# Linear attention: q formed transposed with its norm applied at the output rows, and x (Wv W_out) computed beside k

## The chip, the cores and the metric

The kernel runs on one core of a Trainium2 chip. A core has a matrix engine (TensorE, PE in the profile; PEld is its loading of weights), a vector engine (VectorE, DVE), an activation engine (ScalarE, ACT), GpSimd (POOL), and SyncE (SP), which here issues DMAs. Each engine takes its instructions in a fixed order and waits on semaphores for the others. Products land in PSUM[...]. The metric is the device time of one execution in microseconds.

## The reference

The program is a small vision tower on four images: a tokenizer, which gives 784 distinct rows of 256 channels per image (each row appears three times in the output), softmax attention across images, a mixture of six experts with two chosen per row, then linear attention, and a second mixture of experts. The change touches only the linear attention of layer 1. It computes, for x the layer norm of h:

```python
qkv = x @ W_qkv + b_qkv
q, k, v = jnp.split(qkv, 3, axis=2)
q = q - jnp.mean(q, axis=2, keepdims=True)
k = k - jnp.mean(k, axis=2, keepdims=True)
q2 = q * q
k2 = k * k
q2s = jnp.sum(q2, axis=2, keepdims=True)
k2s = jnp.sum(k2, axis=2, keepdims=True)
k2 = _l2_normalize(k2 / (k2s + EPS_DIV), axis=-2)
q2 = _l2_normalize(q2 / (q2s + EPS_DIV), axis=-1)
kv = jnp.einsum('bnc,bnd->bcd', k2, v)
t2 = jnp.einsum('bnc,bcd->bnd', q2, kv) / math.sqrt(N)
attn = v + t2
return attn @ W_out + b_out        # and then h = h + this
```

The norm of k2 runs over the rows of an image, that of q2 over the channels of one row.

## The kernel before

All arithmetic is fp32. The 784 rows of an image are 7 tiles of 112 rows; a unit is 4 or 3 tiles of one image, so there are eight units (0 to 7), two per image. h holds all 28 tiles in SBUF.

The expert stage ahead of the linear attention processes 30 blocks of 256 rows, one after another: each is fetched, transposed (turned), taken through two hidden layers (hidden) and written back to DRAM (rows_back). In its later part, the loop at L1483, VectorE and SyncE run in the order in which the code is written (manual_schedule); the other engines, and everything after that loop, are ordered by the compiler's scheduler at build time. centred_weights (L623) subtracts from the q and k weights and biases their means over the output channels, so that q and k need no mean subtracted later; it is called inside that loop.

For linear attention, fetch(u) (L1406) gathers each row's two expert results with indirect DMAs, issued by POOL, into one of three ys buffers. stats_one (L1423) adds them, weighted, to h and takes mean and variance; normalise (L1441) makes the normalised rows xa, and, once the weights of layer 1 exist, adds the output bias to h (residual, L1459). x_t (L1465) transposes xa to lxT: channels on the partitions, rows along the free dimension. copy_out (L77) gives the copies out of PSUM in turn to ScalarE and VectorE.

q_k (L1604) multiplies lxT by the q and k weights, 512 columns at a time, rows on the partitions (pqk); VectorE adds the bias, ScalarE squares both halves in place and sums each row, and squares q's half once more into a scratch tile (junk) for the sum of q's fourth powers. scales (L1637) turns the sums into factors: uk is k's squares scaled, and q's squares are scaled in place on VectorE. fold (L1660) adds up the squares of uk over rows. q_t (L1671) transposes the scaled q squares to lqT. k_x (L1676) forms k's product with x (pukx) and the norm over rows (pn), and scales the product to g; g_t transposes it and kv_out (L1714) multiplies it by Wvo, so that kvo holds kv @ W_out. rows_out (L1728) accumulates x @ Wvo and lqT @ kvo in one PSUM bank (pout) and adds the result to h.

Wvo = Wv @ W_out, its bias bvo and the output bias are made by layer1_weights (L639): four transposes (pwv), a copy to WvT by VectorE, two products (pwvo) copied by ScalarE, and one for the bias (pbvo). It is called in the loop at L1751, in step u = 1. That loop runs over the units in a pipeline: step u handles q and k of unit u, k_x and kv_out of the image that is complete, rows_out of unit u - 2, and the statistics of unit u + 1.

## Time and profile before

| | us |
|---|---|
| median of 3 runs | 810.28 |
| lowest and highest run | 808.37, 810.49 |
| profiled execution | 810.54 |
| its span, first to last instruction | 808.8 |
| linear attention, first product to last (pqk at 501.38 to the end of pout) | 162.1 |
| TensorE busy in the span | 739.7 |

The profile is of one execution. It lists, for each engine, busy time and instructions; stretches of time show where an engine is full; the groups name the line, the engine, the tiles written and read, the shape and the count, and then what ended the idle time before them. A TensorE product in fp32 is listed as two instructions, so that 28 tiles of pqk with two products each appear as 112. Groups of the linear attention, by shape, in 470 to 665 us of the span (busy us, mean ns, then idle time before):

```profile
L1620 PE MATMUL pqk<-Wqkv,lxT 128*112 128x512 f32 x112 | 49.7, 594 | 0.5 <-ACT lxT L81 0.5
L1735 PE MATMUL pout<-Wvo,lxT 128*112 128x256 f32 x112 | 29.0, 380 | 0.0
L1740 PE MATMUL pout<-kvo,lqT 128*112 128x256 f32 x112 | 28.8, 380 | 0.0
L1694 PE MATMUL pukx<-xa,uk 112*128 112x258 f32 x112 | 25.9, 384 | 0.0
L300 PE MATMUL pt<-ident,qk 112*128 112x112 f32 x56 | 7.0, 268 | 0.0
...
L1429 DVE SCALAR_TENSOR_TENSOR h<-ys,wk,h 112x256 f32<-112x256 f32 x48 | 21.8, 467 | 3.7 <-DMA ys<-yrows,pos 3.6
L1624 DVE TENSOR_TENSOR qk<-pqk,bqkv 112x512 f32<-112x512 f32 x28 | 19.1, 685 | 9.2 <-PE pqk L1620 9.1
L1653 DVE TENSOR_SCALAR qk<-qk,ss 112x256 f32<-112x256 f32 x28 | 8.4, 360 | 0.1
L1746 DVE TENSOR_TENSOR h<-pout,h 112x512 f32<-112x512 f32 x12 | 8.2, 685 | 8.5 <-PE pout L1740 8.5
...
L1628 ACT ACTIVATE qk<-qk 112x256 f32<-112x256 f32 x56 | 22.8, 407 | 27.7 <-DVE qk L1624 25.2 <-DMA yrows<-yb 2.3
L1629 ACT ACTIVATE junk<-qk 112x256 f32<-112x256 f32 x28 | 11.2, 400 | 0.0
```

A mean of one instruction holds its whole latency; neighbours on an engine overlap, so the distance from start to start is shorter than the duration listed.

### The profile page before, as it was taken

Reading aid. Unit: us, or ns where it says so; the run is one execution under the profiler, and the core shown is the slowest. Engines: PE = TensorE matmul, PEld = TensorE weight load, DVE = VectorE, ACT = ScalarE, POOL = GpSimd, SP = SyncE. Lnnn points to the kernel's source line nnn. Section 1 sums busy time; section 2 is a strip of 40 time slices with the busy share of each in tenths; the row PEclk is TensorE's granted clock in tenths of the full one; section 3 lists DMA queues with packets and bytes.
Section 4 is the critical chain, followed back from the end, with each engine's and each line's share of the span. In section 5 each row is a group of like instructions: output and inputs, shape, how many; then the busy total and the mean of one; then the engine's idle time right before and its main releaser. Section 6 shows DMA issues by size and latency. Waiting matters only on the chain. (4 is left out here: it accounts for less than half of the span.)

```text
span 808.8 us, 10871 instructions
## 1 busy us (share of the span) xinstructions
PE 739.7 (91%) x3524; PEld 501.2 (62%) x3524; DVE 504.0 (62%) x1618; ACT 334.1 (41%) x789; POOL 131.0 (16%) x148
## 2 busy tenths in 40 slices
PE   5779996999788887999999999799999999999996
PEld 3645554555555655887888887475776775555553
DVE  4618776586767986546445746699975655554441
ACT  0326776355376475443222322527544503222221
POOL 4100000000006350760012030775000000000000
PEclk9889997999999988999999999899999999999999
DMA  8999991000002167442334334232000003333333
GB/s 204 371 419 421 420 420 46 1 0 1 1 0 63 36 225 237 143 147 92 105 97 132 94 109 128 85 87 69 1 1 1 1 20 89 90 94 94 94 91 90
DMA packets 58183, 97.39 MB, mean 120 GB/s; under 512 B 14519, under 2 KB 48494, under 8 KB 53262
## 3 DMA queue, kind: packets, MB, share of 16 engines
q1 hardware_dynamic: 50832, 80.52, 28.9%
q0 software_dynamic: 6112, 14.01, 6.0%
q10 hardware_dynamic: 1182, 2.16, 1.1%
q8 instruction: 28, 0.46, 0.2%
q14 instruction: 29, 0.24, 0.1%
HBM read 30.93 MB, written 65.74 MB: 120 GB/s over the span
## 5 line engine op out<-in xcount | busy, mean ns | idle before, releaser
L947 POOL DMA_INDIRECT xrows<-xn,pos x56 | 59.8, 1068 | 274.6 <-ACT kq L711 233.3
L1415 POOL DMA_INDIRECT ys<-yrows,pos x56 | 57.2, 1021 | 141.9 <-DMA yrows<-yb 125.8
L1219 PE MATMUL pb<-xTb,own 128*128 128x256 f32 x240 | 58.8, 389 | 3.8 <-DVE r L810 1.6
L1225 ACT ACTIVATE hb<-pb,own 128x256 f32<-128x256 f32 x74 | 35.1, 475 | 56.2 <-PE pb L1219 47.8
L1219 PE MATMUL pb<-hb,own 128*128 128x256 f32 x240 | 57.1, 380 | 0.3 <-DVE hb L1227 0.3
L1236 PE MATMUL pyb<-own,hb 128*128 128x256 f32 x240 | 57.0, 380 | 0.2 <-ACT hb L1225 0.2
L1219 PEld LDWEIGHTS pb<-xTb,own 128*128 128x128 f32 x240 | 44.6, 194 | 12.5 <-ACT hb L1225 1.9
L517 PE MATMUL pw<-Wall,pT 128*112 128x512 f32 x112 | 51.0, 610 | 0.0
L1620 PE MATMUL pqk<-Wqkv,lxT 128*112 128x512 f32 x112 | 49.7, 594 | 0.5 <-ACT lxT L81 0.5
L1236 PEld LDWEIGHTS pyb<-own,hb 128*128 128x128 f32 x240 | 45.4, 190 | 6.7 <-ACT hb L1225 0.6
L1219 PEld LDWEIGHTS pb<-hb,own 128*128 128x128 f32 x240 | 43.3, 190 | 5.9 <-DVE hb L1227 0.9
L300 PE MATMUL pt<-ident,xn 112*128 112x112 f32 x224 | 34.6, 286 | 12.5 <-DVE xn L540 6.8
L309 PE MATMUL pe<-xT,eW 128*128 128x448 f32 x112 | 45.2, 546 | 0.0
L1242 DVE TENSOR_TENSOR yb<-pyb,eb 128x512 f32<-128x512 f32 x30 | 20.7, 691 | 39.2 <-PE pyb L1236 38.8
L1209 ACT COPY xTb<-ptb 128x512 f32<-128x512 f32 x30 | 17.5, 584 | 64.0 <-PE ptb L1205 64.0
L300 PEld LDWEIGHTS pt<-ident,xn 112*128 112x128 f32 x224 | 27.0, 151 | 26.9 <-ACT xn L824 9.5
L1227 DVE TENSOR_SCALAR hb<-pb,own 128x256 f32<-128x256 f32 x46 | 22.1, 481 | 29.5 <-PE pb L1219 29.5
L517 PEld LDWEIGHTS pw<-Wall,pT 128*112 128x112 f32 x112 | 20.1, 182 | 26.2 <-issue 22.9
L320 PE MATMUL pwo<-Wo,oT 128*112 128x256 f32 x112 | 29.0, 413 | 7.5 <-DVE oT L776 6.7
L736 DVE SCALAR_TENSOR_TENSOR prod<-kq 128x784 f32<-128x784 f32 x32 | 30.3, 969 | 7.4 <-ACT kq L711 5.2
L1620 PEld LDWEIGHTS pqk<-Wqkv,lxT 128*112 128x112 f32 x112 | 19.3, 177 | 24.8 <-issue 23.0
L1628 ACT ACTIVATE qk<-qk 112x256 f32<-112x256 f32 x56 | 22.8, 407 | 27.7 <-DVE qk L1624 25.2
(360 smaller groups left out, 1502.6 us busy)
## 6 DMA issues: line engine op xcount, KB each, us to landing
xrows<-nothing SPq DMA_DIRECT2D x19, 1024.0 KB, 20.2
yrows<-nothing SPq DMA_DIRECT2D x19, 1024.0 KB
out_dram<-h SPq DMA_DIRECT2D x26, 336.0 KB, 3.8
xb<-xrows SPq DMA_DIRECT2D x30, 256.0 KB, 2.7
yrows<-yb SPq DMA_DIRECT2D x30, 256.0 KB, 2.2
ew<-in_L_ffn_expert_w_dram SPq DMA_DIRECT2D x6, 768.0 KB, 11.4
wb<-wd SPq DMA_DIRECT2D x28, 112.0 KB, 3.5
img<-in_x_dram SPq DMA_DIRECT2D x2, 588.0 KB
```

What stands on the lines that cost most here:

```text
L300: nc.tensor.transpose(pt[:, j * TT : (j + 1) * TT], xn[:, j, c * P : (c + 1) * P], ident[:TT, :TT])
L309: nc.tensor.matmul(pm[: wcols.stop - wcols.start, :n], w[:, c, wcols], xT(c), start=(c == 0), stop=(c == chunks - 1),)
L320: nc.tensor.matmul(pm[:, i, :], xT(c, t), w[:, c, :], start=(c == 0), stop=(c == chunks - 1))
L517: nc.tensor.matmul(pm, pTf[:, c, cut(t0 + j, 1)], Wall[:, c, :], start=(c == 0), stop=(c == 1))
L736: nc.vector.scalar_tensor_tensor(prod, qTs[s][:, o, :], 1.0, kT[:, o, t * SEQ : (t + 1) * SEQ], ALU.mult, ALU.mult, accum_out=atts[s][:, o ...
L947: put = nc.gpsimd.indirect_dma_start(out=xrows[:, :], out_offset=bass.IndirectOffsetOnAxis(ap=pos[:, k, t0 + j : t0 + j + 1], axis=0), in_ ...
L1219: nc.tensor.matmul(pm, wm[:, c, o * P : (o + 1) * P], src[:, c, :], start=(c == 0), stop=(c == 1),)
L1225: nc.scalar.activation(dst[:, o, :], pm, AF.Relu, bias=b)
L1236: nc.tensor.matmul(pm[:, t, :], src[:, c, t * P : (t + 1) * P], wm[:, c, :], start=(c == 0), stop=(c == 1),)
L1415: got = nc.gpsimd.indirect_dma_start(out=y[:, j, k, :], out_offset=None, in_=yrows[:, :], in_offset=bass.IndirectOffsetOnAxis(ap=pos[:, k, ...
L1620: nc.tensor.matmul(pqk, xT[:, c, cut(j, 1)], Wqkv[:, c, : 2 * D], start=(c == 0), stop=(c == 1),)
L1628: nc.scalar.activation(half, half, AF.Square, accum_out=ss[:, j, i : i + 1])
```

## The change

q is no longer formed beside k. q_of(u) forms it transposed, the weights standing still and the rows moving, two products of up to 448 columns for each half of the channels; ScalarE adds the bias column bq as it squares the result into lqT, and squares that again into q4. norms(u) sums q4 over the channels with a stationary block of 32 columns of ones (pq4, one column group per tile), copies the sums to qn, turns them into columns by a product with a strided view of the identity (pqn), and takes the reciprocal of the root (rq). It is called one step later than q_of. q's squares stay unscaled: rows_out multiplies the product with kvo by rq as it adds it to h (pqo).

k_of(u) forms k alone in unit 0. From unit 1 on, Wvo stands in the place of the v weights in Wqkv, so k and x @ Wvo come out of one product of 512 columns (pk); VectorE adds the first half to the bias and the second half to h. Unit 0 makes x @ Wvo in rows_out (pxo).

layer1_weights is called at the end of step 0 and copies WvT on ScalarE. The columns of bv (bvs) and of q's bias (pbq, bq) are made inside the block loop. The statistics of unit 2 and later are taken after k of the whole unit; a dependency that orders without a semaphore puts the adds of stats_one behind the last reciprocal of scales(1) for unit 2, and then behind the last add of the unit before. q_t, the junk tile and the scaling of q's squares are gone.

The diff, cut to its core:

```diff
...
-    def layer1_weights():
+    def q_bias():
+        pb = ps_tile("pbq")
+        for c in range(2):
+            nc.tensor.matmul(
+                pb[:, c : c + 1], bqkv[:1, c * P : (c + 1) * P], ones[:1], start=True, stop=True
+            )
+        return pb
+    def bias_columns():
+        bvs = w1p.tile([P, 2, P], F32, tag="bvs", name="bvs")
+        for k in range(2):
+            nc.vector.tensor_copy(bvs[:, k, :], col("bv", k).to_broadcast([P, P]))
+        return bvs
+    def layer1_weights(bvs):
         WvT = w1p.tile([P, 2, D], F32, tag="WvT", name="WvT")
         pt = ps_tile("pwv").rearrange("p (k i) -> p k i", k=2)
         for k in range(2):
...
-        nc.vector.tensor_copy(WvT, pt)
-        Wvo = w1p.tile([P, 2, D], F32, tag="Wvo", name="Wvo")
+        nc.scalar.copy(WvT, pt)
+        Wvo = Wqkv[:, :, 2 * D :]
...
-        bvs = w1p.tile([P, 2, P], F32, tag="bvs", name="bvs")
-        for k in range(2):
-            nc.vector.tensor_copy(bvs[:, k, :], col("bv", k).to_broadcast([P, P]))
...
+    bq = w1p.tile([P, 2], F32, tag="bq", name="bq")
...
     lw = []
+    behind = []
     def stats_one(u, j):
...
         for k in range(2):
-            nc.vector.scalar_tensor_tensor(
+            got = nc.vector.scalar_tensor_tensor(
                 h[:, t, :], ys[u][:, j, k, :], wk[:, k, t : t + 1], h[:, t, :],
                 ALU.mult, ALU.add,
             )
+            for name in behind if u > 1 else ():
+                tc.add_manual_dep(
+                    got.ins, name,
+                    mybir.DependencyInfo(
+                        mybir.DependencyClass.NoSync, mybir.DependencyReason.DATA
+                    ),
+                    reason="order",
+                )
+        if u > 1 and j == units[u][2] - 1:
+            behind[:] = [got.ins.name]
...
                 hidden(i, 1)
             if i == NEARLY + 1:
                 centred_weights()
+                bvs = bias_columns()
+            if i == NEARLY + 3:
+                pbq = q_bias()
+            if i == NEARLY + 5:
+                nc.vector.tensor_copy(bq, pbq[:, :2])
             for u in range(3):
                 if i - 1 == after[u]:
                     fetch(u)
...
     late = [early]
     lin = linear.enter_context(tc.tile_pool(name="lin", bufs=2, reuse_waits="tile"))
-    sumsof = {}
-    def q_k(u, j0, j1):
+    sumsof, q4s, rqs, with_v = {}, {}, {}, set()
+    ones32 = lin.tile([P, 32], F32, tag="ones32", name="ones32", bufs=1)
+    nc.vector.memset(ones32, 1.0)
+    def k_of(u):
+        b, j0, n = units[u]
+        if lw:
+            with_v.add(u)
+        xT = xTs[u]
+        kr = qks[u] = lin.tile([TT, GT, D], F32, tag="kr", name="kr")
+        ss = sumsof[u] = small.tile([TT, GT], F32, tag="ss", name="ss")
+        for two in halves(range(n)):
+            if not lw:
+                pk = mm_rows(two, lambda c, j: xT[:, c, cut(j, 1)], Wqkv[:, :, D : 2 * D], "pk")
+                nc.vector.tensor_tensor(
+                    kr[:, two[0] : two[-1] + 1, :], pk, over(bqkv[:, D : 2 * D], len(two)),
+                    ALU.add,
+                )
+            for j in two:
+                if lw:
+                    pk = ps_tile("pk")[:TT]
+                    for c in range(2):
+                        nc.tensor.matmul(
+                            pk, xT[:, c, cut(j, 1)], Wqkv[:, c, D:], start=(c == 0), stop=(c == 1)
+                        )
+                    nc.vector.tensor_tensor(kr[:, j, :], pk[:, :D], bqkv[:, D : 2 * D], ALU.add)
+                    ht = h[:, b * TPI + j0 + j, :]
+                    nc.vector.tensor_tensor(ht, pk[:, D:], ht, ALU.add)
+                nc.scalar.activation(
+                    kr[:, j, :], kr[:, j, :], AF.Square, accum_out=ss[:, j : j + 1]
+                )
+                if u > 1:
+                    stats_one(u + 1, j)
+        if u > 1:
+            next_stats(u)
+    def next_stats(u):
         n = units[u][2]
...
+        if u == 1:
+            for j in range(n):
                 stats_one(u + 1, j)
-        if j1 >= n and u:
+        if u:
             if u + 1 < len(units) and units[u + 1][2] > n:
                 stats_one(u + 1, n)
             normalise(u + 1)
+    def q_of(u):
+        n = units[u][2]
+        qT = qTs[u] = lin.tile([P, 2, GN], F32, tag="lqT", name="lqT", bufs=3)
+        q4 = q4s[u] = lin.tile([P, 2, GN], F32, tag="q4", name="q4", bufs=2)
+        for o in range(2):
+            pq = mm_t(
+                n * TT, Wqkv, slice(o * P, (o + 1) * P), lambda c: xTs[u][:, c, : n * TT], "pq1"
+            )
+            nc.scalar.activation(qT[:, o, : n * TT], pq, AF.Square, bias=bq[:, o : o + 1])
+        nc.scalar.activation(q4[:, :, : n * TT], qT[:, :, : n * TT], AF.Square)
+    def norms(u):
+        n = units[u][2]
+        q4 = q4s.pop(u)
+        pg = psum_s.tile([P, 512], F32, tag="pss", name="pq4")[: 32 * n, :TT]
+        for c in range(2):
+            for j in range(n):
+                nc.tensor.matmul(
+                    pg[32 * j : 32 * (j + 1), :], ones32, q4[:, c, cut(j, 1)],
+                    start=(c == 0), stop=(c == 1),
+                )
+        qn = small.tile([P, TT], F32, tag="qn", name="qn", bufs=2)[: 32 * n]
+        nc.scalar.copy(qn, pg)
+        pr = psum_s.tile([P, 512], F32, tag="pss", name="pqn")[:TT, :n]
+        nc.tensor.matmul(
+            pr, qn, ident.rearrange("p (j e) -> p j e", e=32)[: 32 * n, :n, 0],
+            start=True, stop=True,
+        )
+        r = rqs[u] = small.tile([TT, GT], F32, tag="rq", name="rq", bufs=4)
+        nc.scalar.activation(r[:, :n], pr, AF.Sqrt, bias=zero[:TT])
+        nc.vector.tensor_scalar(r[:, :n], r[:, :n], 1e-19, None, ALU.max)
+        nc.vector.reciprocal(r[:, :n], r[:, :n])
     def scales(u):
         b, j0, n = units[u]
-        qk = qks[u]
-        ss, s4 = sumsof.pop(u)
+        kr = qks.pop(u)
+        ss = sumsof.pop(u)
         nc.vector.tensor_scalar(ss[:, :n], ss[:, :n], 1e-7, None, ALU.add)
-        nc.scalar.activation(s4[:, :n], s4[:, :n], AF.Sqrt, bias=zero[:TT])
-        nc.vector.scalar_tensor_tensor(
-            ss[:, :n, 0], ss[:, :n, 0], 1e-12, s4[:, :n], ALU.mult, ALU.max
-        )
-        nc.vector.reciprocal(ss[:, :n], ss[:, :n])
+        last = nc.vector.reciprocal(ss[:, :n], ss[:, :n])
+        if u == 1:
+            behind.append(last.ins.name)
         uk = uks[u] = lin.tile([TT, GT, D], F32, tag="uk", name="uk", bufs=3)
         sq = lin.tile([TT, GT, D], F32, tag="sq", name="sq", bufs=1)
         for j in range(n):
-            nc.scalar.activation(uk[:, j, :], qk[:, j, D:], AF.Copy, scale=ss[:, j, 1:2])
-            nc.vector.tensor_scalar(
-                qk[:, j, :D], qk[:, j, :D], ss[:, j, 0:1], None, ALU.mult
-            )
+            nc.scalar.activation(uk[:, j, :], kr[:, j, :], AF.Copy, scale=ss[:, j : j + 1])
         for j in range(n):
             nc.scalar.activation(sq[:, j, :], uk[:, j, :], AF.Square)
...
-    def q_t(u):
-        n = units[u][2]
-        qT = qTs[u] = lin.tile([P, 2, GN], F32, tag="lqT", name="lqT", bufs=3)
-        transposed(qks.pop(u), n, lambda c, pt: copy_out(qT[:, c, : n * TT], pt))
...
     def rows_out(u):
         b, j0, n = units[u]
-        xT, qT, kvo = xTs.pop(u), qTs.pop(u), kvos[b]
+        xT, qT, kvo, r = xTs.pop(u), qTs.pop(u), kvos[b], rqs.pop(u)
         for two in halves(range(n)):
...
             t = b * TPI + j0 + two[0]
             ht = h[:, t : t + len(two), :]
-            nc.vector.tensor_tensor(ht, pm[:, : len(two), :], ht, ALU.add)
+            if u not in with_v:
+                pm = mm_rows(two, lambda c, j: xT[:, c, cut(j, 1)], Wvo, "pxo")
+                nc.vector.tensor_tensor(ht, pm, ht, ALU.add)
+            pq = mm_rows(two, lambda c, j: qT[:, c, cut(j, 1)], kvo, "pqo")
+            for i, j in enumerate(two):
+                nc.vector.scalar_tensor_tensor(
+                    ht[:, i, :], pq[:, i, :], r[:, j : j + 1], ht[:, i, :], ALU.mult, ALU.add
+                )
...
         if u == 0:
             fetch(3)
             x_t(1)
-            q_k(0, 0, GT)
+            k_of(0)
+            q_of(0)
             squares[0] = scales(0)
             fold(0, squares.pop(0))
+            lw.extend(layer1_weights(bvs))
+            Wvo, bvo = lw[:2]
             continue
         if u < len(units):
             fetch(u + 3)
...
             shared = shared1(0)
         if one_image:
             k_x(b)
-            q_t(u - 1)
+        if u == len(units):
+            norms(u - 1)
         if u == 2:
...
         if u < len(units):
-            q_k(u, 0, 2)
+            k_of(u)
         if one_image and b:
             gT = g_t(b)
         if u < len(units):
-            q_k(u, 2, GT)
+            q_of(u)
+            norms(u - 1)
+            squares[u] = scales(u)
             if u == 1:
-                lw.extend(layer1_weights())
-                Wvo, bvo = lw[:2]
-            squares[u] = scales(u)
+                next_stats(u)
         if one_image and b:
             kv_out(b, gT)
         if u == len(units) - 1:
...
         if 2 <= u < len(units) - 1:
             x_t(u + 1)
         if u == 3:
-            for k in range(3):
+            for k in range(2):
                 residual(k)
...
             fold(u, squares.pop(u))
-            if u % 2:
-                q_t(u - 1)
```

## The prediction

> **What bounds the kernel now.** I read the share of busy time first, then the busy time by stretch of the linear-attention stage (the only stage the change rewrites), the TensorE timeline at its start, the chain that ended last, and the groups by shape.

> ```profile
> PE 739.7 (91%) x3524; PEld 501.2 (62%) x3524; DVE 504.0 (62%) x1618; ACT 334.1 (41%) x789; POOL 131.0 (16%) x148
> ...
> 501.38:545.37 43.99, 36.87 (x145) 25.20 (x143) 35.15 (x100) 18.69 (x69) 31.02 (x31) 0.92 0.30 85
> 545.37:663.47 118.10, 117.27 (x520) 81.54 (x521) 87.86 (x268) 57.61 (x207) 11.44 (x11) 1.00 0.05 13
> ...
> 550.00:575.00 25.00, 24.76 (x108) 16.59 (x107) 24.48 (x75) 15.43 (x59) 7.72 (x9) 1.00 0.15 42
> 600.00:625.00 25.00, 24.99 (x115) 18.18 (x114) 12.68 (x38) 10.97 (x40) 0.00 (x0) 1.00 0.00 1
> ...
> 520.00:522.00 2.00, 2.00 (x5) 1.62 (x6) 2.00 (x9) 1.14 (x7) 1.47 (x2) 0.50 0.24 72
> 532.00:534.00 2.00, 1.63 (x11) 1.24 (x10) 1.73 (x7) 0.85 (x3) 1.70 (x2) 1.00 0.36 109
> 534.00:536.00 2.00, 1.26 (x7) 0.81 (x7) 2.00 (x6) 0.59 (x1) 1.39 (x3) 1.00 0.21 64
> ...
> 501.38 12.18 PE L1620 MATMUL pqk<-Wqkv,lxT 128*112 128x512 f32 x28
> 513.40 0.60 PE L644 MATMUL pwv<-ident,Wqkv 128*128 128x128 f32 x4
> 519.77 3.78 PE L653 MATMUL pwvo<-Wout,WvT 128*128 128x256 f32 x8 [5.77 <-DVE WvT L648]
> ...
> 507.86 0.48 DVE L1429 SCALAR_TENSOR_TENSOR h<-ys,wk,h 112x256 f32<-112x256 f32 x1 [2.15 <-DMA ys<-yrows,pos]
> 519.04 0.68 DVE L648 COPY WvT<-pwv 128x512 f32<-128x512 f32 x1
> ...
> 580.01 1.73 PE pkvo L1720 x8
> 581.74 0.58 PE pt L300 x6
> 582.31 0.87 PE pout L1735 x4
> 583.18 0.86 PE pout L1740 x4
> 589.22 5.15 PE pqk L1620 x12
> 638.02 3.02 PE ps L309 x8
> 667.26 0.52 PE pgate L1559 x16
> ```

> The columns of a stretch are busy time of PE, PEld, DVE, ACT, POOL, then the clock, the DMA share and GB/s. From 545.37 to 663.47 us TensorE idles 0.83 of 118.1 us: it is the bound, and the chain there is TensorE almost alone. VectorE is nearly full until 600 (24.48 of 25), half empty after. Before 545.37 TensorE idles 7.1 of 44 us, 5.77 of it for one copy of WvT, which stands on VectorE behind the statistics of unit 2, whose rows POOL is still gathering.

> [...] the clock is 0.50 at 520 to 522, after the 5.77 us hole, and 1.00 at 532 to 536, where the holes are short. [...] 532 to 536, mostly transposes, kept the clock, with 0.7 us of true products in it. [...]

> **Prices.** Each fp32 product appears as two passes; a transpose as one. From the chain: 512 columns 5.15/12 = 0.429 us a pass; 256 columns 0.216 (0.86/4); 448 columns 3.02/8 = 0.378, hence 336 about 0.284; a 112-column transpose 0.58/6 = 0.096; the 32-column products of the norm by pgate, 0.52 for four tiles.

> **TensorE work.** Per image of 7 tiles, before: q beside k 28 passes, 12.0 us; 14 transposes of q 1.35; x Wvo 28 x 0.216 = 6.05; sum 19.4. After: x Wvo beside k 12.0; q transposed 8 x 0.378 + 8 x 0.284 = 5.3; norms 0.52 + 0.45, and two small products (pqn) at half of pn's four passes (0.49), 0.25 each: 1.5; sum 18.8. So only 0.6 us an image goes; kvo products stay. Unit 0 keeps its separate x Wvo, at the same price.

> **VectorE and ScalarE.** Start to start, an add of 112x512 takes 0.60 us, of 112x256 0.34, a scaled add from PSUM 0.40. Per image: before qk adds 4.2, q scaled 2.0, lqT copies 0.95, output adds 2.1; after two adds a tile 4.8, output 7 x 0.40 = 2.8, norm scalars 0.3. That is 7.9 against 9.3. ScalarE drops 21 squares (0.40 each) to 7 and gains the q squares (0.55 each, by the 0.634 activation of 128x448), q4 [...] and the qn copy (0.25). Neither binds by its sum.

> **A. Block stage.** pbq is two products of one column (ptotal shows 0.14 for two passes): +0.28, TensorE being full there. The bvs copies (2 x 0.14 start to start) leave 310 us, where the next VectorE step waits for a DMA anyway, and join centred_weights, where TensorE already waits 0.33 and 0.53 for VectorE: +0.28. The bq copy lies in VectorE's idle 1.2 us a block. Bounds 0 to +0.8; I take +0.5. pbq holds one of seven PSUM banks for two blocks; six serve a block (one ptb, four pb, one pyb), so I charge nothing, 0.2 if a product has to wait. POOL's last gathers move with the stage.

> **B. Start of the stage, walked in the changed kernel's issue order, times on before's clock.** TensorE: k of unit 0 501.4 to 504.8, q to 507.9, pwv to 508.3. ScalarE: four squares from 504.0, q's two squares when their products land (506.5, 508.05), uk, q4 until 509.9, sq of four tiles, then WvT 511.5 to 512.1: strict order, so it now stands behind ScalarE's own work, not behind a gather. TensorE idles 1.7, does the norm sums (0.6), idles 1.5, does pwvo and pbvo to 514.7 at full clock, k and x of unit 1 to 519.9, q, then pukx until 528.4. VectorE, freed of statistics so far, finishes residual and the unit-1 scales at 522.0 and only then starts unit 2's statistics: 8 scaled adds of unit 2 and 2 of unit 3 (0.385 each), 4 bn_stats (0.335), 4 of xa (0.325), the fold (0.60 + 2 x 0.335) and small ones (0.6) sum to 8.4 us, so acc is ready at 530.4 (before, 530.8) and xa of unit 2 at 530 (before, 522.7, needed only at 543). pn 530.5, kn, residual, g 533.2, gT 534.3, pkvo 536.1, rows_out(0) 543.05, x_t(2), k of unit 2 at 544.2 against 545.37: -1.1. The cold clock (0.44 us for a 256-column pass, 3.0 us lost over 519 to 526) and the hole go, but unit 1's x (12 passes, 2.6 us) and q of units 0 and 1 come in, and VectorE's serial 8.4 us caps the gain. POOL doesn't suffer: ys has three buffers, unit 5's gathers (533) need unit 2's adds (done 527), unit 7's (553) those of unit 4 (551). SP's queue keeps its order.

> **C. From unit 2 to the end.** Three images at -0.6, and unit 1's x done already: -1.8 - 2.6 = -4.4. New waits: at unit 3, TensorE finishes x_t(3) at 554.7 but the norm sums of unit 2 stand next and need q4, which ScalarE reaches at 556.5 (second q square 554.6 to 555.2, one uk, q4); then k of unit 3 needs the lxT copy that ScalarE has queued behind four sq: 558.1. That is 1.9 + 1.0 us, less 0.5 for two lxT waits of 0.24 that go. Later units have rows_out or other products between x_t and k, so the copy hides; pqn waits for qn some 0.15 to 0.2, twice; at the end gT stands behind the norm's square root (0.3). Sum +2.9, bounds +1 to +5. rows_out's two adds per pair are covered by the pass rate (0.86 a tile against 0.40 + 0.34).

> **Sum.** +0.5 - 1.1 - 4.4 + 2.9 = -2.1. The profiled span is 808.8, its run 810.54 (1.7 us around the span), 0.26 above the median 810.28. So 808.2.

> **Rivals.**
> 1. The clock goes cold in the start all the same: between 507.9 and 512.1 only 0.6 us of narrow products run. For: transposes at 312 to 314 didn't keep the clock. [...] Price: pwvo 3.57 instead of 1.73, pbvo +0.5: +2.3, so 810.5.
> 2. The unit-3 wait is absent (q4 or lxT in time), or the start gains its whole hole: -2.1 - 2.9 = -5.0, 805.3. For: 0.429 us passes may leave ScalarE further ahead than I have it. Against: the queue order is fixed.
> 3. VectorE becomes the bound, slower. Tying statistics behind scales moves 6.1 us of VectorE work (8 scaled adds, 4 bn_stats and bn_aggr, xa of unit 2) from 508 to 522 into a stretch already 24.48 of 25 full; if none is recovered before 600, x_t(3), x_t(4) and PSUM banks come late: -2.1 + 6.1 = +4.0, 814.3. It decides once TensorE waits over 2.1 us more in all for VectorE between 545 and 600. Against: the change takes 1.4 us an image and the early qk work off VectorE.

> **Chances.** Forecast 0.55, rival 1 0.09, rival 2 0.20, rival 3 0.16. The forecast's own range is 806 to 810.5. A measurement tells about 0.3%, 2.4 us, from no change: the line is 807.85. Faster: half of the forecast (0.28) and rival 2, 0.48. Slower (over 812.7): most of rival 3 and a little else, 0.15. Same: 0.37. Range for eight in ten: 804.0 to 812.5, leaving out the far part of rival 3.

> **What would show it.** Right: no TensorE hole over 2.2 us between 507 and 535, clock 1.00 throughout, pwvo passes at 0.216; k of unit 2 starting about 544.7; two holes of 1.9 and 1.0 us around the norm sums before k of unit 3; the stage ending about 661. Wrong: a clock of 0.5 after 512 (rival 1), k of unit 3 following x_t(3) at once (2), or TensorE waits on kr, h or xa (3). A changed block or expert stage, beyond 0.8 us, would contradict all of it.

## The result and the profile after

The changed kernel takes 812.82 us (median; 811.24 to 814.03), the kernel before beside it 808.14 (805.93 to 810.49): a ratio of 1.0052, 95% interval [1.0035, 1.0070]. It is slower, by 4.7 us between the medians; 808.2 was forecast.

The profiled execution (span 811.4 us), busy time by stretch: from the first product of the stage to k of unit 2, then to the second group of the experts' transposes. Columns as before: busy PE, PEld, DVE, ACT, POOL, then clock, DMA share, GB/s.

```profile
PE 739.4 (91%) x3568; PEld 495.4 (61%) x3568; DVE 493.7 (61%) x1621; ACT 327.5 (40%) x708; POOL 134.0 (17%) x148
...
500.13:548.30 48.17, 41.70 (x179) 29.68 (x177) 29.82 (x87) 16.39 (x47) 34.22 (x33) 0.86 0.29 83
548.30:665.98 117.68, 114.77 (x525) 73.08 (x526) 84.78 (x284) 49.73 (x142) 10.71 (x9) 0.99 0.04 11
```

The second stretch shrank, from 117.94 us (545.37 to 663.31, the same two events before) to 117.68. The loss is in the first: 48.17 us against 43.99. Its clock is 0.86, against 0.92 before, although the long hole is gone.

TensorE's timeline of the changed kernel at the places that the forecast named (start, duration, group, idle time before it):

```profile
508.71 0.59 PE L1704 MATMUL pq<-q,ones 128*32 128x112 f32 x16 [1.52 <-ACT q L1694]
510.80 3.66 PE L668 MATMUL pwvo<-Wout,WvT 128*128 128x256 f32 x8 [1.50 <-ACT WvT L663]
514.30 1.03 PE L676 MATMUL pbvo<-Wout,bvs 128*128 128x256 f32 x4
...
530.87 0.66 PE L1753 MATMUL pn<-ones,acc 112*128 112x1 f32 x4 [1.83 <-DVE acc L1746]
...
535.36 3.78 PE L1792 MATMUL pkvo<-Wqkv,gT 128*128 128x256 f32 x8 [0.68 <-ACT gT L1783]
538.94 3.17 PE L320 MATMUL pxo<-Wqkv,lxT 128*112 128x256 f32 x8
...
560.60 0.59 PE L1704 MATMUL pq<-q,ones 128*32 128x112 f32 x16 [1.59 <-ACT q L1694]
562.14 7.01 PE L1659 MATMUL pk<-Wqkv,lxT 128*112 128x512 f32 x12 [0.96 <-ACT lxT L81]
```

The holes are those forecast: 1.52 and 1.50 us in the start (1.7 and 1.5), 1.59 and 0.96 around the norm sums before k of unit 3 (1.9 and 1.0), none over 2.2. But four groups behind them last too long. Eight passes of 256 columns take 3.66, 3.78 and 3.17 us (1.97 to 1.99 at full clock in the filled kernel's profile below), and twelve of 512 take 7.01 (5.40 there).

The same execution cut at the places where its clock changes, which lie 3.41 us or a multiple of it apart:

```profile
507.39:510.80 3.41, 0.59 (x16) 0.35 (x17) 0.49 (x1) 3.41 (x10) 2.50 (x4) 1.00 0.29 84
510.80:514.21 3.41, 3.41 (x8) 2.78 (x9) 0.20 (x1) 0.47 (x2) 2.80 (x3) 0.50 0.32 94
...
527.87:531.28 3.41, 1.58 (x10) 1.10 (x8) 3.41 (x12) 0.30 (x1) 2.80 (x3) 1.00 0.30 90
531.28:534.69 3.41, 2.70 (x20) 1.81 (x19) 3.41 (x11) 0.77 (x3) 2.80 (x3) 0.50 0.11 34
534.69:538.11 3.42, 2.75 (x7) 2.19 (x8) 1.97 (x9) 0.62 (x2) 2.50 (x4) 0.50 0.34 101
538.11:541.52 3.41, 3.41 (x10) 2.47 (x9) 1.91 (x6) 0.27 (x1) 2.80 (x3) 0.50 0.35 101
...
558.59:562.00 3.41, 1.00 (x21) 0.55 (x19) 3.41 (x9) 3.41 (x10) 2.74 (x2) 1.00 0.21 59
562.00:565.41 3.41, 3.27 (x4) 1.37 (x5) 2.17 (x8) 0.54 (x3) 0.00 (x0) 0.50 0.13 38
```

Read the first busy figure of a line against the clock of the next. After 0.59, 1.58 and 1.00 us of work in a window, the next one runs at 0.50. Five windows at half clock withhold 5 x 3.41 x 0.5 = 8.5 us of TensorE's full speed. In the kernel before, one hole of 5.77 us, which left a whole window empty, cost two such windows, 3.4 us:

```profile
515.55:518.96 3.41, 0.00 (x0) 0.00 (x0) 3.41 (x9) 3.41 (x14) 2.50 (x4) 1.00 0.31 91
518.96:522.37 3.41, 2.60 (x6) 2.16 (x7) 3.41 (x13) 2.44 (x11) 2.80 (x3) 0.50 0.34 97
522.37:525.79 3.42, 3.42 (x11) 2.69 (x11) 0.86 (x5) 0.37 (x1) 2.50 (x4) 0.50 0.27 77
```

The difference, 5.1 us, is of the size of the loss. What it costs in time has to come from experiments.

### The profile page after: what moved, and what is told of

Read it like the earlier page. It is cut to its first block, busy times and chain, and to the rows that moved or that the text cites. A ratio compares the mean times of both kernels' runs of the same rounds, so it can differ in the third digit from the quotient of the medians.

```text
span 811.4 us, 10883 instructions
## 1 busy us (share of the span) xinstructions
PE 739.4 (91%) x3568; PEld 495.4 (61%) x3568; DVE 493.7 (61%) x1621; ACT 327.5 (40%) x708; POOL 134.0 (17%) x148
## 4 chain that ended last, share of the span: by engine, by line
PE 74%; DVE 11%; ACT 6%; issue 3%; DMA 2%; POOL 2%; SPq 1%; DVEq 0%; ACTq 0%; POOLq 0%
PE pb L1231 12%; PE pw L517 6%; PE pyb L1248 6%; PE pkv L309 5%; PE pe L309 5%; PE pk L1659 5%; PE ps L309 4%; PE pqo L320 3%; PE ps L1921 3%; PE pwp L320 3%; PE pt L300 3%; PE pq L309 2%; PE pukx L1766 2%; DVE oT L783 2%; PE ptp L356 2%
## 5 line engine op out<-in xcount | busy, mean ns | idle before, releaser
L1432 POOL DMA_INDIRECT ys<-yrows,pos x56 | 59.6, 1065 | 143.5 <-DMA yrows<-yb 127.3
L1659 PE MATMUL pk<-Wqkv,lxT 128*112 128x512 f32 x96 | 44.1, 612 | 1.2 <-ACT lxT L81 1.2
L309 PE MATMUL pe<-xT,eW 128*128 128x448 f32 x112 | 45.2, 546 | 0.0
L300 PE MATMUL pt<-ident,xn 112*128 112x112 f32 x224 | 34.2, 285 | 11.8 <-DVE xn L540 6.8
L300 PEld LDWEIGHTS pt<-ident,xn 112*128 112x128 f32 x224 | 26.8, 151 | 25.7 <-ACT xn L836 8.7
L309 PEld LDWEIGHTS pe<-xT,eW 128*128 128x128 f32 x112 | 20.2, 190 | 20.9 <-issue 20.9
L1208 DVE COPY own<-ew 128x1540 f32 x30 | 28.9, 963 | 5.3 <-issue 1.8
```

The lines of the kernel that those rows point to most:

```text
L300: nc.tensor.transpose(pt[:, j * TT : (j + 1) * TT], xn[:, j, c * P : (c + 1) * P], ident[:TT, :TT])
L309: nc.tensor.matmul(pm[: wcols.stop - wcols.start, :n], w[:, c, wcols], xT(c), start=(c == 0), stop=(c == chunks - 1),)
L1208: nc.vector.tensor_copy(w, ewf[0][:, bass.ds(off, EW)])
L1432: got = nc.gpsimd.indirect_dma_start(out=y[:, j, k, :], out_offset=None, in_=yrows[:, :], in_offset=bass.IndirectOffsetOnAxis(ap=pos[:, k, ...
L1659: nc.tensor.matmul(pk, xT[:, c, cut(j, 1)], Wqkv[:, c, D:], start=(c == 0), stop=(c == 1))
```

## The experiments

Theory: only the clock makes the change slow; TensorE falls to half speed after every 3.41 us window in which it is busy for less than about half (17, 46 and 29% in the windows above). Rivals: the holes and waits are the loss in themselves; the tied statistics make VectorE the bound.

Each ratio is to the kernel before, run beside the experiment. The sessions were of two kinds. In some, that of the result among them, that kernel took 808 us; in three, 846 to 853 us, and the profiles taken there show engines standing still during GpSimd's gathers. ScalarE's timeline in the first run of the version called `best2` below shows it:

```profile
533.73 0.75 ACT L1704 ACTIVATE q<-lqT 128x672 f32<-128x672 f32 x1
551.88 0.25 ACT L1719 COPY qn<-pq 128x112 f32<-128x112 f32 x1 [17.40 <-remote]
```

A copy whose input was ready near 531.5 us starts only at 551.88, after ScalarE has stood still for 17.4 us. In an undisturbed session the same copy of the same kernel follows without a wait. What the engine waits for is not known. Ratios are compared within one kind of session only, and the verdicts below rest on the undisturbed ones.

| run | undisturbed (before 808 us) | with stalls (before 846 to 853 us) |
|---|---|---|
| changed kernel | 1.0052, 1.0049 [1.0035, 1.0064] | 0.9981 [0.9961, 1.0001] |
| wide filler, small holes too | 0.9985 [0.9973, 0.9998] | 0.9933 [0.9918, 0.9949] |
| narrow filler, small holes too | 0.9982 [0.9968, 0.9996] | - |
| weights in the block stage | 0.9965 [0.9950, 0.9979] | 0.9953, 0.9920 |
| fold first | 1.0063 [1.0039, 1.0087] | 0.9935 |
| no tie | 1.0068 [1.0042, 1.0095] | 1.0171, 1.0150 |
| holes filled with needed work | 0.9915 [0.9890, 0.9941] | 0.9933 [0.9910, 0.9956] |

**Holes filled with throwaway products.** The filler multiplies two resident matrices into a bank that nobody reads, chained between the products around a hole. It adds work and leaves none out; the products around the holes are written out in the order that the changed kernel's trace shows, so that the chain holds.

```diff
+    def filler(prev, *cols):
+        for n in cols:
+            pd = ps_tile("pfill")
+            got = nc.tensor.matmul(
+                pd[:128, :n], ident[:, :128], Wqkv[:, 0, :n], start=True, stop=True
+            )
+            prev = behind_of(got, prev)
...
         nc.scalar.copy(WvT, pt)
+        got = filler(norms(0, filler(got, *(512, 256))), *(512, 256))
```

The first set ran with stalls. Wide filler:

> The changed kernel with throwaway products (ident x Wqkv, 128 output rows, 512 or 256 columns, never read) put into its three TensorE holes: 1.29 us each side of the norm sums of unit 0, 1.72 us before pn of image 0, 1.29 us before and 0.86 us after the norm sums of unit 2, where the trace of the changed kernel shows holes of 1.52, 1.50, 1.83, 1.59 and 0.96 us. Nothing else moves. Clock theory (the changed kernel is slower only because TensorE falls to half clock in three spells; pwvo 3.50, pkvo 3.78, pxo 3.01, k of unit 3 6.85 us instead of 1.73, 1.73, 1.73, 5.15): the clock stays 1.00 over all of it, the stage takes 159 to 161 us instead of 165.85, and the ratio to before is 0.998 (0.996 to 1.000). Rival (the time is lost in the holes and in the waits on VectorE and ScalarE themselves): extra products in idle time give nothing, ratio 1.004 to 1.007.

Narrow filler:

> The same throwaway products in the same places and of the same length, but with 32 output rows instead of 128 (a quarter of the array's columns). If what keeps the clock is that TensorE has work in time, this equals the wide filler: ratio 0.998, clock 1.00. If what counts is how much of the array works (the reading of the changed kernel's trace, where 0.59 us of narrow norm products kept nothing), the clock falls as in the changed kernel: clock 0.50 in the same three places and ratio 1.004 to 1.007.

Filler in the start only:

> Wide throwaway products only around the norm sums of unit 0, before pwvo. Clock theory: the first spell goes (pwvo 3.50 to 1.73 us), the ones at pkvo and at k of unit 3 stay, so 1.8 to 2.5 us less than the changed kernel: ratio 1.0025 (1.001 to 1.004). Rival (holes themselves): 1.004 to 1.007.

Measured: 0.9950, 0.9961 and 0.9972, with intervals of about 0.002 either side. Their order fits the clock, but with stalls the changed kernel alone is at 0.9981, so they settle little. The wide filler still had half clock at pkvo, behind a window with the small products and small holes around pn. So the next version fills those too.

> As the wide filler, and with throwaway wide products also in the small holes between pn and pkvo of image 0 (256 columns before and after the norm sums of unit 1, 512 before pkvo), about 8.2 us of throwaway work in holes of about 8.8 us. Clock theory: no half clock anywhere in the stage, so 5 to 7 us less than the changed kernel of this call: ratio to it 0.992 to 0.994, to before 0.997 to 0.999. Rival (holes and waits themselves are the loss): equal to the changed kernel or up to 0.5 us slower.

Measured: 0.9933 against 0.9981, 3.7 us by the medians, with stalls. Without:

> The changed kernel once more, as the anchor of this call. If engines don't stall while GpSimd gathers (kernel before near 808 us): every theory expects 1.0035 to 1.007 and half clock in three places. If they do (kernel before near 846): 0.996 to 1.000 as in the call before.

> All holes of the start, of image 0's norm and of unit 3 filled with throwaway wide products, as in the call before, where it took 0.5% less than the changed kernel (0.9933 against 0.9981 to before). Clock theory: again 4 to 7 us less than the changed kernel of this call; without engine stalls the profile shows clock 1.00 through the whole stage, pwvo 1.73, pkvo 1.73, k of unit 3 5.15 us, and the ratio to before is 0.997 to 0.999. Rival (holes and waits themselves): within 0.5 us of the changed kernel.

Measured: 1.0049 and 0.9985, so 5.0 us less (811.71 to 806.70) with more work to do. The profile of the filled kernel:

```profile
502.73:545.71 42.98, 42.33 (x196) 28.73 (x194) 29.73 (x87) 16.41 (x47) 30.00 (x29) 1.00 0.28 81
545.71:661.78 116.07, 115.42 (x530) 73.45 (x531) 84.80 (x284) 49.77 (x142) 13.54 (x14) 1.00 0.06 16
...
513.40 1.99 PE L694 MATMUL pwvo<-Wout,WvT 128*128 128x256 f32 x8
...
535.83 1.97 PE L1849 MATMUL pkvo<-Wqkv,gT 128*128 128x256 f32 x8
...
559.56 5.40 PE L1687 MATMUL pk<-Wqkv,lxT 128*112 128x512 f32 x12
```

The clock is 1.00 throughout, the three groups have their full speed, and the start takes 42.98 us instead of 48.17. It is not the order that changed: in both kernels pwvo starts 10.67 us after the stage's first product, and of the 5.2 us between the two starts pwvo makes 1.7, the stretch from pn to pkvo 0.5, pkvo 1.8 and pxo 1.3. Nor are the holes what makes the kernel slower than before: throwaway products stand in them and the stage is shorter. That the clock does is shown.

> The same throwaway products at the same places and of the same lengths, with 32 output rows instead of 128. If TensorE being busy in time is what keeps the clock, this equals the wide filler to 1 us. If the part of the array that works counts, half clock stays in at least two of the three places and the time is that of the changed kernel (4 us or more above the wide filler). The first narrow run, in stalled runs, was within 1.7 us of the wide one and kept the clock at pwvo, so I lean to time.

Measured: 0.9982, clock 1.00. The quarter-width filler does as well as the wide one. My reading that the norm sums "kept nothing" because they are narrow is wrong: there were too few of them.

**The start alone.** All of `layer1_weights` moves into the block stage.

```diff
+            if i == NEARLY + 9:
+                made = layer1_weights(bvs)
+            if i == NEARLY + 11:
+                layer1_bias(made)
...
-            lw.extend(layer1_weights(bvs))
+            lw.extend((made[0], made[1], bout))
```

> The changed kernel with the whole of layer1_weights (transposes of W_v, W_v W_out, bias product, copies) taken into the block stage beside the bias columns, eight blocks further; the same work, done where TensorE has no holes (3.2 us more there). Clock theory: the holes of 1.52 and 1.50 us and the half-clock pwvo (1.77 us too long) go, the two later spells stay: 4 to 5 us less than the changed kernel, ratio to before 0.999 to 1.001. Rival (VectorE's serial work from the scales of unit 1 to acc and the gathers of unit 2 cap the start): less than 2 us less, because the time comes back as a longer hole before pn.

> layer1_weights in the block stage, again. Without stalls: ratio 0.999 to 1.001 (theory: start's holes and half clock at pwvo go), rival (time comes back before pn) 1.003 or more. With stalls: 0.991 to 0.996 as before.

Measured: 0.9965 undisturbed, about 6.8 us under the changed kernel (0.0084 of 808, across two sessions), more than the 4 to 5 expected. TensorE's timeline says why:

```profile
517.76 0.59 PE L1711 MATMUL pq<-q,ones 128*32 128x112 f32 x16
...
524.69 0.50 PE L1760 MATMUL pn<-ones,acc 112*128 112x1 f32 x4
...
528.54 0.94 PE L1787 MATMUL pgT<-ident,g 128*128 128x128 f32 x4 [1.69 <-DVE g L1777]
```

The start's holes are gone, the norm sums stand between other products, and the hole before pn is gone as well: pn starts 20.9 us after the stage's first product, in the changed kernel 30.7. Half clock is down to one window, behind the 1.69 us before pgT. The start takes 37.79 us: 10.4 less, of which some 3.1 were only moved (pwv, pwvo and pbvo, from start to start in the filled kernel).

**The fold first.** Unit 1's fold is written ahead of unit 2's statistics.

```diff
             if u == 1:
+                fold(u, squares.pop(u))
                 next_stats(u)
...
-        if u < len(units):
+        if u < len(units) and u > 1:
             fold(u, squares.pop(u))
```

> The changed kernel with the fold of unit 1 written ahead of the statistics of unit 2, so that VectorE makes acc about 3 us earlier and pn of image 0 no longer waits; nothing is moved on the start and little in unit 3. Theory (that hole leaves a clock window less than half busy): the hole of 1.83 us goes and with it half clock at pkvo and pxo, 3 to 5 us less than the changed kernel, ratio 0.999 to 1.002. Rival (xa of unit 2, which is now later, or VectorE's serial work sets the time anyway): within 1.5 us of the changed kernel, 1.003 to 1.006.

> The fold of unit 1 ahead of the statistics of unit 2, again, because engines stalled during gathers in the call before (kernel before 852 us). Without stalls: the hole of 1.83 us before pn and half clock at pkvo and pxo go, ratio 0.999 to 1.002; rival (VectorE's serial work sets the time anyway) 1.003 to 1.006. With stalls: 0.992 to 0.995 as before.

Measured: 1.0063; the theory's number is missed. The hole moved instead of going, as windows and timeline of this run show:

```profile
531.98:535.39 3.41, 1.73 (x18) 0.88 (x16) 3.41 (x14) 0.81 (x3) 2.80 (x3) 1.00 0.34 101
535.39:538.81 3.42, 2.71 (x7) 2.00 (x8) 2.36 (x5) 0.59 (x1) 2.55 (x3) 0.50 0.22 67
...
535.42 0.90 PE L1780 MATMUL pgT<-ident,g 128*128 128x128 f32 x3 [1.35 <-DVE g L1770]
537.00 3.78 PE L1792 MATMUL pkvo<-Wqkv,gT 128*128 128x256 f32 x8 [0.68 <-ACT gT L1783]
```

pn no longer waits, but g does, behind statistics and xa of unit 2 on a VectorE that is full for all 3.41 us. The small holes now fall into one window with 1.73 us of work, and pkvo runs at half clock as in the changed kernel. Six windows of this profile's stage are at half clock. With stalls the same edit gave 0.9935.

**Without the tie.** stats_one goes over an empty list instead of `behind`, so that no statistics are tied; nothing else is edited.

> The changed kernel without the order that ties the statistics of a unit behind the scales before it: VectorE takes unit 2's scaled adds and statistics in the start again, as their rows land. Theory of the clock: the tie costs only through the hole of 1.83 us before pn of image 0 (acc stands behind 8.4 us of VectorE work) and the spell that follows it at pkvo and pxo (3.3 us); without it the hole and that spell go, but VectorE steps behind a late gather can delay WvT's followers: ratio 1.001 (0.998 to 1.005), with the spells at pwvo and at k of unit 3 unchanged. Rival (VectorE is the bound of units 2 to 5 because of the tie): TensorE waits for VectorE between 545 and 600 disappear and the stage gains 4 us or more there, ratio 1.000 or less with the clock as it was.

> Without the tie of the statistics, again. Without stalls: theory 1.002 to 1.008, the start's holes larger and the one before pn smaller; rival (the tie is what makes the change slow) 1.000 or less. With stalls: 1.014 to 1.018 as twice before.

Measured: 1.0068, no better than the changed kernel. The start of this run:

```profile
508.81 0.97 PE L1704 MATMUL pq<-q,ones 128*32 128x112 f32 x16 [3.83 <-ACT q L1694]
511.29 3.45 PE L668 MATMUL pwvo<-Wout,WvT 128*128 128x256 f32 x8 [1.51 <-ACT WvT L663]
...
517.42 1.11 PE L1659 MATMUL pk<-Wqkv,lxT 128*112 128x512 f32 x2 [1.81 <-ACT Wqkv L672]
```

Without the tie the start's holes grow from 1.52, 1.50 and none to 3.83, 1.51 and 1.81 us. The rival that the tie is what makes the change slow falls; with stalls the kernel without it is 1.7 to 1.9% slower than the changed kernel. The profile is that of the fastest of six executions (810.46 us; median 814.22). It has only two windows at half clock, 3.4 us as before, but TensorE idles 13.7 of the stage's 165.3 us, against 9.4 of 165.9 in the changed kernel. So here it is the holes themselves that cost.

**Holes filled with needed work** (`best2`). The weights in the block stage; x Wvo of unit 0 ahead of pn; the fold first; unit 1's output products between the transposes and k of unit 3, both of whose copies go to VectorE; the residual of units 0 to 2 at unit 5.

```diff
+        if b == 0:
+            x_out(0)
         pn = psum_s.tile([P, 512], F32, tag="pss", name="pn")
...
             x_t(u + 1)
+        if u == 2:
+            rows_out(1)
...
-        if u >= 2 and (b or odd):
+        if u > 3:
             rows_out(u - 2)
```

> A version that fills the holes with work that is needed: layer1_weights in the block stage as in the run beside it; x Wvo of unit 0 (8 passes) ahead of pn; the fold of unit 1 ahead of the statistics of unit 2; the output products of unit 1 between the transposes and k of unit 3, whose transposed rows are both copied by VectorE; the residual bias of units 0 to 2 added at unit 5. Clock theory: start -4.8, hole before pn and spell at pkvo and pxo -4, unit 3 -2.3 of holes and -1.7 of half clock: 10 to 13 us less than the changed kernel, ratio to before 0.988 to 0.993. Rival (VectorE caps the start and units 2 and 3): 0.996 to 1.000.

> The version that fills the holes with needed work. Clock theory: 10 to 13 us less than the changed kernel, ratio to before 0.988 to 0.993 if engines don't stall; in stalled runs, where ScalarE stands still for 17 us at its first copy of the norm sums, only 4 to 6 us less. Rival (VectorE's serial work caps the start): less than 6 us less than the changed kernel even without stalls.

Measured: 0.9915 undisturbed (801.21 us), 10.5 us under the changed kernel and 6.5 under the kernel before: inside the expected 10 to 13, and faster than both. One window at half clock is left, behind a wait of 1.15 us for g. These are five edits in one; apart from the weights, what each is worth was not measured.

**How full a window must be.** The changed kernel's second profiled execution has the same holes on another grid of windows:

```profile
506.67:510.08 3.41, 1.46 (x22) 0.74 (x20) 0.00 (x0) 3.41 (x9) 2.75 (x3) 1.00 0.34 101
510.08:513.49 3.41, 2.34 (x6) 1.89 (x7) 0.69 (x1) 1.40 (x5) 2.55 (x3) 0.50 0.32 89
...
557.87:561.28 3.41, 1.81 (x25) 1.18 (x23) 3.41 (x10) 3.41 (x9) 2.67 (x2) 1.00 0.23 67
561.28:564.69 3.41, 2.45 (x17) 0.99 (x8) 3.41 (x11) 1.60 (x6) 0.00 (x0) 1.00 0.12 38
```

Here pwvo is slow for two windows instead of one. Before k of unit 3 the holes of 1.60 and 0.96 us fall into two windows, 1.81 and 2.45 us busy, and the clock stays. That execution needs 116.08 us from k of unit 2 to the end, the first one 117.68.

Busy time as recorded is only a rough measure of fullness, because a record holds an instruction's whole latency: a transpose set off alone is listed with 0.31 us, in a row they follow each other every 0.096 us. In the kernel before, the window from 228.84 us on is 69% busy, nearly all of it with such transposes, and half clock follows; the one from 256.15 on, 71% busy with wide products, keeps the clock. An estimate that counts columns instead (columns of the moving operand: 0.429 us for a pass of 512, so 0.84 ns each, twice that at half clock; products of 32 output rows, such as the norm sums', at a quarter, since sixteen of them with 112 columns are listed with 0.59 us in all) sorts the windows better: the two above are filled to 29 and 62%. In the profiles of the kernel before and of the changed kernel, from 24 us of the span to 790, half clock followed every window that columns filled to 38% or less and none filled to 41% or more.

## Why the prediction was wrong

**The failed step** is in B: "does pwvo and pbvo to 514.7 at full clock". Half clock in this stage had been seen behind a hole of 5.77 us alone, and the start's holes of 1.7 and 1.5 us were taken for too short to cost it. How short is too short, the trace of before didn't show: in the changed kernel the clock fell after windows of 3.41 us that were 17, 29, 35 and 46% busy. The mechanism of rival 1 came true and was priced too low: it was placed only at pwvo and cost 2.3 us. pwvo took 1.7 us too long, but pkvo, pxo and k of unit 3 followed, 5.1 us of withheld speed more than before. With the windows kept busy, 5.0 us of time came back.

**B otherwise.** At full clock the start takes 42.98 us, 1.0 less than before; 1.1 less was forecast. The holes were forecast to 0.3 us. ScalarE's order held: pwv ends near 507.2 us, and WvT, behind the last sq, starts at 510.18. The time of q4, which no trace of before had shown, is 0.84 us from start to start for 128x896 (507.72 to 508.56).

**C.** From k of unit 2 on, 116.07 us with the holes filled, 116.08 with the holes and a kept clock, 117.94 before: 1.9 less, 1.5 forecast. The unit-3 waits are there (2.6 of 2.9 us), and so are the holes of the start, so rival 2 falls. C's own parts (1.9 + 1.0 - 0.5, 0.3 to 0.4 for pqn, 0.3 at the end) make 3.0 to 3.1 where the prediction has 2.9; that changes nothing.

**Rival 3.** VectorE's serial work is real: pn waits 1.83 us for acc. Counted from the stage's first product, it starts at 29.1 us with the holes filled, as forecast (530.5 less 501.4), and at 30.7 in the changed kernel, behind the slow pwvo. But without the tie nothing is gained, and the changed kernel's one wait of TensorE for VectorE over half a microsecond is that before pn; the experiments moved it to pgT. What makes 1 to 2 us of such a wait dear is the clock.

**A.** With the holes filled, the stage is 2.9 us shorter than before (159.05 against 161.93), and the time only 1.2 us (0.9985), so some 1.7 us would lie outside the stage, where 0.5 was put. The profiles can't settle it. What follows the stage takes 145.4 to 145.8 us in all nine undisturbed ones; the stage begins at 501.38 in the one profile of before, and anywhere from 497.9 to 502.7 in the six of them whose block stage is that of the changed kernel. No run took the bias steps out alone: it stays open.

Open too: what stalls engines during the gathers, and why the change is no loss then (0.9981).

## What to carry to other kernels

Add up TensorE's work over windows, 3.41 us in these runs, instead of looking for the longest hole, and count columns rather than recorded time where the products are small (the window filled to 29% above was recorded as 69% busy). In the start, two holes of 1.5 us around 0.6 us of work took half the speed from the next window, 1.7 us. Before pricing a wait, look at what else is idle near it; if needed work can be put there, or the waiting step moved to where TensorE is full, the clock is won as well as the hole: `best2` kept one window at half clock of five, at 0.9915. A hole that is only shifted by reordering the late engine may take the slow window with it: the fold first had six, at 1.0063.
